# Second layer of a four-layer network: image 0 read and counted ahead, feed-forward and spectrum issued in turns

## The chip, the cores and the metric

The kernel runs on one core of one Trainium2 chip. The metric is device time in microseconds (us) for one execution of the whole network, the median of the timed runs. Five engines work beside each other, each from its own queue: TensorE (PE, with its weight loads listed as PEld), VectorE (DVE), ScalarE (ACT), GpSimd (POOL) and SyncE (SP), which issues most DMAs.

## The reference

Four images of 64 x 64 pixels with 128 channels pass through four layers, each of the form `x = x + layer(group_norm(x))` with 32 groups, all in float32:

```python
def _gn(v, G=32, eps=1e-5):          # mean and variance over pixels and 4 channels
...
x = x + _L0_conv_ref(_gn(x), ...)    # selective scan in four directions over 4096 steps
x = x + _L1_conv_ref(_gn(x), ...)    # the layer of this change
x = x + _L2_conv_ref(_gn(x), ...)    # spectral convolutions with attention over channels
x = x + _L3_conv_ref(_gn(x), ...)    # attention in 7 x 7 windows
```

The second layer takes, along each of the two image axes, a real Fourier transform, keeps 16 modes, multiplies each mode by its own complex 128 x 128 matrix, transforms back, adds the two results, and runs a feed-forward with a layer norm:

```python
def _L1_conv_ref(x, w1, w2, ff_w0, ff_b0, ff_w1, ff_b1, ln_g, ln_b):
    ...
    f1 = jnp.einsum('bixy,ioy->boxy', rfft(xt, axis=-1)[..., :16], cw1)   # axis y
    f2 = jnp.einsum('bixy,iox->boxy', rfft(xt, axis=-2)[:, :, :16], cw2)  # axis x
    h = irfft(f1, axis=-1) + irfft(f2, axis=-2)
    h1 = relu(einsum('bmni,ih->bmnh', h, ff_w0) + ff_b0)                  # 128 to 512
    h2 = einsum('bmnh,ho->bmno', h1, ff_w1) + ff_b1                       # 512 to 128
    return layer_norm(h2, ln_g, ln_b)
```

(The transforms are shown in short; they are unitary, norm 'ortho'.)

## The kernel before

**Layer 0** (`layer0`) takes 73% of the time. Its work is cut into 128 units: 4 images, 4 scan directions, 8 chunks of 512 steps. A unit has 16 steps, one for each state, of about 2.75 us: POOL multiplies `dB`, ACT makes `dA`, DVE scans into `h`, PE transposes `h` (`pt`), ACT copies it (`hT`), and PE multiplies it with `W` into `yT`. PE runs seven steps behind (`LAG`), so after the last unit a loop drains the queue (`while queue or copied: transposed()()`). The order on PE, ACT, DVE and POOL is the order of the program (`tc.manual_schedule`); SP's is left to the scheduler. Work on the side (`Side`) is put into fixed steps: `before` prepares the next image, `after` closes an image in eight bands of 512 pixels. A band reads the summed `y` and the gate `z` back from DRAM (`yf`, `zf`), normalizes, transposes (`pg`), scales (`yg`), multiplies by `z` on POOL, projects (`op`), adds the residual (`xr`) and stores `x1`. The last band of image 3 can begin only when the drain has ended, and it runs in `d.finish`.

**Layer 1** (`layer1`, `layer1_image`) is written image by image; the scheduler orders all engines by its own model, within the limits of the buffers. Its pools are opened when those of layer 0 are released. For each image:

- `load_image` reads x in four DMAs (two buffers `x1`), and `group_norm` makes 32 transposes (`gn_ps`), 8 `bn_stats`, and two small matmuls (`gn_gm`, `gn_gv`) that give scale and offset.
- For each axis: 32 matmuls `pu` with the 96 columns of the transform, copied by ACT with the scale into `U`; 64 matmuls `pg` with `w1` or `w2`, copied by DVE into `G`; 16 transposes `pt`, copied by ACT into `GT`; 16 matmuls `ph`, which DVE copies into `hT` (axis 0) or adds to it (axis 1). Axis 1 uses `xa`, the same image read from DRAM in the other order. `U`, `G`, `xa` and `hT` have one buffer each.
- The feed-forward, in 8 chunks of 512 pixels: 4 matmuls `pf` with bias and relu on ACT (`h1`), 16 matmuls `po`, then layer norm on DVE (`h2`), the sum into x and a store.

In float32 each matmul appears twice in the profile, as two passes, and a transpose once. After image 0, `layer2_weights` loads and combines constants of layer 2. Layers 2 and 3 follow and are not touched, but the pools of layer 2 lie where those of layer 1 lay. L1067 is the helper line through which all of layer 2 is issued.

Of the kernel before, what the change touches and what calls it, by code (L numbers as in the profile page):

```python
# [84 lines left out]
def layer0(sh, A, x_in, x_out, scr):  # L85
# [7 lines left out]
    with ExitStack() as ctx:  # L93
# [28 lines left out]
        xds = [wp.tile([65, CH], F32, name=f"xd{n}") for n in range(2)]  # L122
        for xd in xds:
            nc.vector.memset(xd, 0.0)
            nc.vector.memset(xd[64:65, :], 1.0)
# [12 lines left out]
        zeros = wp.tile([P, WD // P], F32, name="zeros")  # L138
        nc.vector.memset(zeros, 0.0)
# [50 lines left out]
        def opening(bank, steps):  # L190

            waiting = {"dve": [], "act": []}
# [25 lines left out]
            pair = lambda name: tmp.tile([P, 2, CH], F32, name=name, tag="t4", bufs=4)  # L218
            whole = lambda: tmp.tile([P, 2, CH, 4], F32, name="h", bufs=3).rearrange("p s t n -> p (s t n)")
            x = whole().rearrange("p (j d) -> p j d", d=DM)  # L220
            for c in range(NCH):
                nc.sync.dma_start(x[:, 4 * c : 4 * c + 4, :], tiles(x_in(0)[c * CH : (c + 1) * CH, :]))
            for name in ("W00", "W01", "W10", "W11"):
                for g in range(4):
                    nc.sync.dma_start(scr(name)[g].rearrange("(p f) -> p f", p=P), zeros)
# [148 lines left out]

        def after(b, st, later, bands):

            for c in bands:
                yield "l"
                rows = slice(c * CH, (c + 1) * CH)
                y = tmp.tile([P, 4, 2 * P], F32, name="yf", tag="t4", bufs=4)  # L380
                nc.sync.dma_start(y, tiles(scr(f"y2{b % 2}")[rows, :]))
# [38 lines left out]
        def residual(b, rows, xr, op):  # L420
            nc.vector.tensor_tensor(xr, xr, op, ALU.add)
            nc.sync.dma_start(tiles(x_out(b)[rows, :]), xr)
# [10 lines left out]
        def inputs(k, c, u, par, spare):  # L433

            xd, bd, Wd = xds[c % 2], scr(f"B{(NCH * k + c) % 3}"), scr(f"W{k // 2}{par}")
# [13 lines left out]
            def blocks():  # L449
                Ct = tmp.tile([48, 32, 16], F32, name="Ct")[32:48]  # L450
# [95 lines left out]
        def products(G, q, hT):  # L546
# [30 lines left out]
            if G["g"] == 3 and q % 2:  # L577
# [10 lines left out]
                if q == 3:  # L588
                    nc.sync.dma_start(U["dst"](k), y)
# [43 lines left out]
        with tc.manual_schedule(engines=order):  # L633
# [4 lines left out]
            for i, (b, k, c) in enumerate(units):  # L638
# [13 lines left out]
                unit = dict(k=k, pos=pos, rev=rev, pc=pc, u=u, yT=[None, None], started=set(), st=ln_st, dst=dst)  # L652
# [7 lines left out]

                for n in range(NS):
# [74 lines left out]
                elif b == NB - 1 and i % per == 3 * per // 4:  # L736

                    done = [NS * (i + 1 + n) + 8 for n in range(NCH)]
                    sides.append(Side(after(b, ln_st, later, range(NCH - 1, -1, -1)), 8 * 6, done[0], 1, done))
            while queue or copied:  # L740
                transposed()()
# [35 lines left out]
def layer1_weights(sh, A, wp):  # L777
# [3 lines left out]
    nc.scalar.dma_start(w["an"], A["c_an1"])  # L781
    for name in ("w1", "w2"):
        w[name] = wp.tile([P, 16, 2, P], F32, name=name)
        nc.sync.dma_start(w[name], A[name])
    w["ff0"] = wp.tile([P, 4, P], F32, name="ff0")
    nc.scalar.dma_start(w["ff0"], A["ff_w0"].rearrange("i (f k) -> i f k", k=P))
    w["ff1"] = wp.tile([P, 4, P], F32, name="ff1")
    nc.scalar.dma_start(w["ff1"], A["ff_w1"].rearrange("(f k) o -> k f o", k=P))
    w["b0"] = wp.tile([P, 4], F32, name="b0")
    nc.scalar.dma_start(w["b0"], A["ff_b0"])  # L790
    w["rows"] = wp.tile([P, 3, P], F32, name="rows1")
    nc.scalar.dma_start(w["rows"], A["l1_rows"].partition_broadcast(P))
    w["sy"] = wp.tile([P, 256], F32, name="c_sy1")
# [4 lines left out]
def layer1_image(sh, w, pools, x_dram, x_out, x=None):  # L798

    nc = sh.nc  # L800
    big, tmp, small, ps = pools
    if x is None:
        x = big.tile([P, NJ, DM], F32, name="x1")
        load_image(nc, x, x_dram)
    s_, o_ = sh.group_norm(lambda j: x[:, j, :], ps, small, tag="a")
# [3 lines left out]
    hT = big.tile([P, NT], F32, name="hT", bufs=1)  # L809
    for axis in range(2):  # L810

        if axis == 0:
            xa = x
        else:
            xa = big.tile([P, NJ, DM], F32, name="xa", bufs=1)
            xv = x_dram.rearrange("(h w2 w1) d -> w1 h w2 d", w1=2, w2=32)
            for q in range(2):
                nc.sync.dma_start(xa[64 * q : 64 * q + 64], xv[q])
        U = tmp.tile([P, 3, 16, 64], F32, name="U1", bufs=1)
        for g in range(NJ // 4):  # L820
# [8 lines left out]
            )  # L829
        nc.vector.tensor_scalar(U[:, 1, 0, :], U[:, 1, 0, :], o8, None, ALU.add)  # L830

        G = tmp.tile([P, 64, 16, 2], F32, name="G1", bufs=1)
        wm = w["w1"] if axis == 0 else w["w2"]
        for g in range(4):
# [5 lines left out]
            nc.vector.tensor_copy(G.rearrange("p l m c -> p m c l")[:, 4 * g : 4 * g + 4], pg)  # L840

        for g in range(4):
# [4 lines left out]
            GT = tmp.tile([P, 4, P], F32, name="GT1")  # L847
            nc.scalar.copy(GT, pt)
            for q in range(0, 4, 2):
# [13 lines left out]
                else:  # L863
                    hv = hv.rearrange("p h w -> p w h")[:, l0 : l0 + 8, :]
                    nc.vector.tensor_tensor(hv, hv, ph, ALU.add)


    for c in range(NCH):
        h1 = tmp.tile([P, 4, CH], F32, name="h1")
        for f in range(4):  # L870
            pf = ps.tile([P, CH], F32, name="pf", tag="a")
            nc.tensor.matmul(pf, lhsT=w["ff0"][:, f, :], rhs=hT[:, c * CH : (c + 1) * CH], start=True, stop=True)  # L872
            nc.scalar.activation(h1[:, f, :], pf, AF.Relu, bias=w["b0"][:, f : f + 1])  # L873
        po = ps.tile([P, 4, DM], F32, name="po", tag="b")
# [6 lines left out]
        h2 = tmp.tile([P, 4, DM], F32, name="h2")  # L881
# [15 lines left out]
        nc.sync.dma_start(x_out[c * CH : (c + 1) * CH, :].rearrange("(j p) d -> p j d", p=P), xc)  # L897


def load_image(nc, x, x_dram):  # L900
    for q in range(4):
        nc.sync.dma_start(
            x[:, 8 * q : 8 * q + 8, :], x_dram[1024 * q : 1024 * q + 1024, :].rearrange("(j p) d -> p j d", p=P)
        )


def layer1(sh, A, x_in, x_out, l2w, wt):

    tc, nc = sh.tc, sh.nc
    with ExitStack() as ctx:  # L910
        pool = lambda name, bufs, **kw: ctx.enter_context(tc.tile_pool(name=name, bufs=bufs, **kw))
        pools = pool("l1big", 2), pool("l1tmp", 2), pool("l1small", 2), pool("l1ps", 4, space=PSUM)
        wp = pool("l1w", 1)
        x = pools[0].tile([P, NJ, DM], F32, name="x1")
        load_image(nc, x, x_in(0))
# [1162 lines left out]
```

## Time and profile before

| | |
|---|---|
| median of 3 timed runs | 7832.24 us (7831.64 to 7838.32) |
| profiled execution, its own time | 7839.47 us |
| span of the profiled instructions | 7837.7 us |
| layer 0: first to last band | 0 to about 5747 us of the span |
| layer 1: image 0's first spectrum matmul | 5783.1 us |
| layer 1: starts of the four feed-forwards | 5841.6, 5969.4, 6095.5, 6221.7 us |
| layer 2: first load of its input | 6284.7 us |
| busy over the whole span | PE 81%, DVE 86%, ACT 78%, POOL 72% |

All times inside the profile are counted from the start of its span. An average over the whole span says little here: layer 0 keeps DVE, ACT and POOL full, and layer 1 is one fifteenth of the time with PE as its busiest engine. So the stages are read one by one.

### The profile page before, as it was taken

The numbers are of one execution on the slowest core, as the hardware profiler recorded it, in microseconds if no ns is written. First come the engines' busy times: TensorE is split into PE (matmuls) and PEld (weight loads), VectorE is DVE, ScalarE is ACT, GpSimd is POOL, SyncE is SP. The second block draws the span as 40 slices with busy tenths as digits, with TensorE's granted clock in tenths as the row PEclk, the third lists the DMA queues.
The fourth block names the chain that finished last, engine by engine and source line by source line (L and its number), as shares of the span: only waits on it lengthen the run. The fifth ranks groups of instructions, "written<-read, shape, count | busy, mean of one in ns | idle before, by whom it ended". The sixth has DMA issues, their size and how long they took to land. (4 is left out here: it accounts for less than half of the span.)

```text
span 7837.7 us, 141040 instructions
## 1 busy us (share of the span) xinstructions
PE 6346.8 (81%) x52796; PEld 4010.0 (51%) x52796; DVE 6755.1 (86%) x8112; ACT 6108.1 (78%) x9714; POOL 5634.8 (72%) x2574
## 2 busy tenths in 40 slices
PE   7888888878888877888887777787768968687789
PEld 3544444444455444445554444454457756464556
DVE  7999999999999999999999999999955556646678
ACT  7999999999999998999999999999832323314667
POOL 4989999989999998999999999999910013123233
PEclk8999999999999999999999999999989979788899
DMA  6555556545556554555555545555542142231332
GB/s 173 171 163 175 177 174 173 175 154 175 187 172 185 181 171 166 166 183 174 185 175 173 172 152 189 176 174 181 175 106 51 29 120 70 70 107 37 103 96 81
DMA packets 1326912, 1159.93 MB, mean 148 GB/s; under 512 B 694165, under 2 KB 1120753, under 8 KB 1259282
## 3 DMA queue, kind: packets, MB, share of 16 engines
q1 hardware_dynamic: 1324546, 1149.16, 47.7%
q8 instruction: 416, 6.82, 0.4%
q14 instruction: 270, 2.21, 0.1%
q10 hardware_dynamic: 1680, 1.74, 0.1%
HBM read 956.89 MB, written 189.74 MB: 146 GB/s over the span
## 5 line engine op out<-in xcount | busy, mean ns | idle before, releaser
L679 DVE TENSOR_TENSOR_SCAN h<-dA,state,dB 128x512 f32<-128x512 f32 x4096 | 4920.4, 1266 | 201.0 <-POOL dB L673 79.8
L673 POOL TENSOR_TENSOR dB<-du,Bb 128x1024 f32<-128x1024 f32 x2048 | 4810.6, 2385 | 338.2 <-DVE h L679 210.6
L533 PE MATMUL pt<-ident,h 128*128 128x128 f32 x16384 | 2221.9, 279 | 878.9 <-ACT hT L543 863.1
L678 ACT ACTIVATE dA<-delta,A_neg 128x512 f32<-128x512 f32 x4096 | 2761.7, 697 | 159.2 <-DVE h L679 131.3
L533 PEld LDWEIGHTS pt<-ident,h 128*128 128x128 f32 x16384 | 1811.4, 142 | 1930.6 <-ACT hT L543 1708.0
L543 ACT COPY hT<-pt 128x1024 f32<-128x1024 f32 x2048 | 2080.1, 1016 | 163.0 <-PE pt L533 145.1
L568 PE MATMUL yT<-hT,W 128*32 128x256 f32 x16384 | 1378.9, 409 | 1.1 <-ACT hT L543 0.6
L568 PEld LDWEIGHTS yT<-hT,W 128*32 128x32 f32 x16384 | 455.4, 150 | 340.6 <-issue 328.1
L1067 POOL COPY XG<-Xs 64x9 f32<-64x9 f32 (+2 forms) x44 | 10.8, 293 | 758.6 <-ACT Xs L1067 758.6
L164 PE MATMUL cv<-xn,taps 128*128 128x512 f32 x936 | 527.0, 644 | 2.8 <-DVE delta L469 2.8
L1798 POOL TENSOR_TENSOR S<-S,sm 128x784 f32<-128x784 f32 x128 | 191.2, 1494 | 417.4 <-DVE sm L1796 248.0
L472 POOL TENSOR_TENSOR du<-delta,u 128x1024 f32<-128x1024 f32 x128 | 304.7, 2380 | 79.5 <-DVE delta L469 79.4
L460 PE MATMUL dp<-xd,w_dt 65*128 65x512 f32 x512 | 288.7, 646 | 68.4 <-ACT Ct L451 45.9
L443 PE MATMUL xd_ps<-u,w_x 128*48 128x512 f32 x512 | 250.1, 611 | 21.4 <-DVE e L361 15.8
L1805 ACT ACTIVATE S<-S,mx 128x196 f32<-128x196 f32 x512 | 227.9, 448 | 35.4 <-DVE mx L1832 34.9
L164 PEld LDWEIGHTS cv<-xn,taps 128*128 128x128 f32 x936 | 139.2, 188 | 180.6 <-issue 160.5
L873 ACT ACTIVATE h<-pf,b 128x512 f32<-128x512 f32 x128 | 88.0, 687 | 144.9 <-PE pf L872 144.9
L469 DVE SCALAR_TENSOR_TENSOR delta<-delta,dp 128x512 f32<-128x512 f32 x256 | 170.7, 667 | 4.1 <-ACT delta L466 1.1
L1760 PE MATMUL pt<-ident,S 128*98 128x128 f32 x1024 | 164.9, 285 | 3.5 <-POOL S L1798 2.0
L466 ACT ACTIVATE delta<-delta 128x512 f32<-128x512 f32 x256 | 166.0, 649 | 0.0
L460 PEld LDWEIGHTS dp<-xd,w_dt 65*128 65x128 f32 x512 | 76.5, 188 | 173.2 <-ACT Ct L451 98.8
L1067 POOL TENSOR_TENSOR WX<-wr,Xs 128x544 f32<-128x544 f32 x40 | 57.3, 1434 | 148.4 <-issue 62.1
(369 smaller groups left out, 7039.3 us busy)
## 6 DMA issues: line engine op xcount, KB each, us to landing
Bb<-l_B SPq DMA_DIRECT2D x512, 1024.0 KB
W<-l_W SPq DMA_DIRECT2D x512, 256.0 KB
l_y<-y SPq DMA_DIRECT2D x128, 512.0 KB
u<-l_xr SPq DMA_DIRECT2D x64, 512.0 KB
u<-l_xw SPq DMA_DIRECT2D x64, 512.0 KB
y<-l_y SPq DMA_DIRECT2D x56, 512.0 KB
V<-l_v SPq DMA_DIRECT2D x512, 49.0 KB
y<-l_y SPq DMA_DIRECT2D x80, 256.0 KB
```

What stands on the lines that cost most here:

```text
L164: nc.tensor.matmul(pm, lhsT=taps[:, s, t, :], rhs=xn[:, dy : dy + 8, dx : dx + 64], start=(t == 0), stop=(t == 8),)
L443: nc.tensor.matmul(bank["x"], lhsT=w_x[:, s, k, :], rhs=u[:, s, :], start=(s == 0), stop=(s == 1))
L460: nc.tensor.matmul(bank[s], lhsT=w_dt[:, k, s * P : (s + 1) * P], rhs=xd, start=True, stop=True)
L472: nc.gpsimd.tensor_tensor(du, delta, u, ALU.mult)
L533: nc.tensor.transpose(pt[:, j, s, :], G["h"][:, s, t0 : t0 + 32, :].rearrange("p t n -> p (t n)"), sh.ident)
L543: return lambda: nc.scalar.copy(hT, pt.rearrange("p j s d -> p j (s d)"))
L568: nc.tensor.matmul(U["yT"][e][32 * jo : 32 * jo + 32, qo % 2, :], lhsT=U["Ws"][G["g"]][:, :, 4 * q + j], rhs=hT[:, j, :], start=((e, jo) n ...
L673: nc.gpsimd.tensor_tensor(dB, du, B_now[:, q : q + 1, :].to_broadcast([P, 2, CH]), ALU.mult)
L678: nc.scalar.activation(dA, delta[:, s, :], AF.Exp, scale=A_neg[:, k, s, n : n + 1])
L679: nc.vector.tensor_tensor_scan(h[:, s, :, q], dA, dB[:, s, :], state[:, s, n : n + 1], ALU.mult, ALU.add)
L1798: nc.gpsimd.tensor_tensor(Sv, Sv, U["sm"].unsqueeze(2).to_broadcast([P, 4, 196]), ALU.mult)
L1805: nc.scalar.activation(Sn, Sn, AF.Exp, bias=U["mx"][:, n : n + 1], accum_out=sm[:, n : n + 1])
```

## The change

Three things are changed; the rest makes room for them.

**Image 0 ahead.** A pool on the right side of SBUF holds the second layer's first image during the whole of layer 0 (16 KB per partition). Its four parts are read at units 116 to 119. The group statistics are made in the drain loop, one chunk a step, and `group_scale` follows ahead of the last band. The last unit's `y` stays in SBUF for the last band instead of going through DRAM, and the last two bands are stored through ACT's queue. To make room, `xd` and `Ct` get one buffer instead of two, and `zeros` shares a buffer with others (tag `t4`).

**Turns.** `layer1_image` becomes two generators: `layer1_spectrum` yields after each small group of matmuls, `layer1_feed` twice per chunk. `layer1` issues the feed-forward of image b - 1 and the spectrum of image b in 16 turns. `hT` gets two buffers, and the feed-forward issues the `pf` of a chunk ahead of the `po` of the one before. SP now keeps the order of the program within layer 1. All pools of layer 1 wait tile by tile for what lay in their place (`reuse_waits="tile"`) and not for a whole pool.

**Layer 2's constants** (`layer2_weights`) become a generator too; it is stepped along with image 2's spectrum instead of following image 0, its tiles lie on the right where image 0 was, and its loads are all on SP.

```diff
-        xds = [wp.tile([65, CH], F32, name=f"xd{n}") for n in range(2)]
+        xd = wp.tile([65, CH], F32, name="xd")
...
-        zeros = wp.tile([P, WD // P], F32, name="zeros")
...
+            zeros = pair("zeros").rearrange("p s t -> p (s t)")[:, : WD // P]
...
+                if kept:
+                    y = kept.pop()
+                else:
+                    y = tmp.tile([P, 4, 2 * P], F32, name="yf", tag="t4", bufs=4)
+                    nc.sync.dma_start(y, tiles(scr(f"y2{b % 2}")[rows, :]))
...
+            eng = nc.scalar if b == NB - 1 and rows.start <= CH else nc.sync
+            eng.dma_start(tiles(x_out(b)[rows, :]), xr)
...
-                Ct = tmp.tile([48, 32, 16], F32, name="Ct")[32:48]
+                Ct = tmp.tile([48, 32, 16], F32, name="Ct", bufs=1)[32:48]
...
-                if q == 3:
+                if q == 3 and U["last"]:
+                    kept.append(y)
+                elif q == 3:
                     nc.sync.dma_start(U["dst"](k), y)
...
+                if len(units) - 12 <= i < len(units) - 8:
+                    load_part(nc, ahead["x"], x_out(0), i - len(units) + 12)
...
+            def count():
+                for c in itertools.islice(counted, 1):
+                    pt = psx.tile([P, CH], F32, name="gn_ps", tag="x")
+                    for q in range(4):
+                        nc.tensor.transpose(pt[:, q * P : (q + 1) * P], ahead["x"][:, 4 * c + q, :], sh.ident)
+                    nc.vector.bn_stats(st[:, c, :], pt)
+
             while queue or copied:
-                transposed()()
+                copy = transposed()
+                count()
+                copy()
+            for c in range(NCH):
+                count()
+            ahead["norm"] = sh.group_scale(st, psx, ahead["pool"], "x", exp_rstd)
             for d in sides:
                 d.finish(flush_all)
...
+    for name, pool in (("w1", wp), ("w2", wq)):
+        w[name] = pool.tile([P, 16, 2, P], F32, name=name)
...
-    hT = big.tile([P, NT], F32, name="hT", bufs=1)
+    hT = out["hT"] = tmp.tile([P, NT], F32, name="hT", bufs=2)
...
+        if axis == 0:
+            out["xa"] = big.tile([P, NJ, DM], F32, name="xa", bufs=1)
+            xv = x_dram.rearrange("(h w2 w1) d -> w1 h w2 d", w1=2, w2=32)
+            for q in range(2):
+                nc.sync.dma_start(out["xa"][64 * q : 64 * q + 64], xv[q])
...
+    h1_next = first(0)
+    for c in range(NCH):
+        h1 = h1_next
+        if c + 1 < NCH:
+            h1_next = first(c + 1)
+        yield
...
+        with tc.manual_schedule(engines=engines):
+            for b in range(NB + 1):
+                out = {}
+                if b < NB:
+                    spectrum = layer1_spectrum(sh, w, pools, x_in(b), x, norm, out)
+                    pieces = 32 + 9 * (norm is None)
+                else:
+                    spectrum, pieces = iter(()), 0
+                turns = 2 * NCH if b > 0 else 1
+                for n in range(turns):
+                    next(fed, None)
+                    for _ in range(pieces * n // turns, pieces * (n + 1) // turns):
+                        next(spectrum)
+                        next(setup, None)
+                for _ in itertools.chain(spectrum, fed):
+                    pass
+                if b < NB:
+                    fed = layer1_feed(sh, w, pools, x, out["hT"], x_out(b))
+                if b == 1:
+                    ahead["close"]()
+                    right = ctx.enter_context(tc.tile_pool(name="l2set", bufs=1, side="right", reuse_waits="tile"))
+                    w2 = {}
+                    setup = layer2_weights(sh, A, l2w, right, pools["ps"], wt, w2)
+                if b + 1 < NB:
+                    x, norm = pools["big"].tile([P, NJ, DM], F32, name="x1", bufs=2), None
+                    load_image(nc, x, x_in(b + 1))
...
+        early = ExitStack()
+        pool = early.enter_context(tc.tile_pool(name="l1x", bufs=1, side="right"))
+        ahead = dict(pool=pool, x=pool.tile([P, NJ, DM], F32, name="x1"), close=early.close)
```

In this code `engines` is SP alone. A spectrum yields 8 times for `pu`, 4 for `pg` and 8 for `pt` and `ph`, for each of two axes, and 9 times for the statistics where it makes them.

## The prediction

> **What bounds the kernel now.** I read the busy table by stages first, cut where the second layer's stages begin, then the chain of waits across the same stretch, then who waited for whom, then the timeline at both ends. Columns of the first view: window, length, then PE, weight loads, DVE, ACT and POOL busy us with their counts, granted clock, DMA share, GB/s.
>
> ```profile
> 5743.20:5783.10 39.90, 12.44 (x52) 10.60 (x53) 9.14 (x23) 1.28 (x1) 0.00 (x0) 0.54 0.93 219
> 5783.10:5841.60 58.50, 50.51 (x354) 46.75 (x354) 35.61 (x79) 13.87 (x25) 0.00 (x0) 0.96 0.61 119
> ...
> 5969.40:6026.10 56.70, 56.69 (x323) 41.15 (x324) 36.96 (x119) 23.20 (x39) 0.00 (x0) 1.00 0.09 29
> 6026.10:6038.00 11.90, 5.15 (x37) 4.17 (x34) 10.32 (x29) 0.30 (x1) 0.00 (x0) 0.82 0.14 44
> 6038.00:6095.50 57.50, 50.73 (x354) 47.18 (x353) 24.28 (x29) 13.86 (x25) 0.00 (x0) 0.95 0.37 74
> 6095.50:6164.10 68.60, 61.85 (x357) 45.34 (x357) 47.27 (x148) 23.49 (x40) 0.00 (x0) 0.97 0.10 31
> ```
>
> The rows are: the gap between the layers (40 us, DMA 93% busy, PE nearly idle); image 0's spectrum; image 1's feed-forward, with PE busy 56.69 of 56.70 us; the turn to image 2, where DVE finishes the feed-forward and the next statistics; image 2's spectrum; its feed-forward and turn. So the layer is one gap and then PE work with small holes: (57.50 - 50.73) + (68.60 - 61.85) = 13.5 us of PE idle in image 2's 126.1 us. DVE is busy 71.6 us of those, ACT 37.4: neither can bind soon.
>
> ```profile
> 5728.10 2.94 DMA l_y<-y
> 5731.06 3.78 DMA yf<-l_y
> ...
> 5758.39 19.64 DMA x<-x
> 5778.16 1.95 PE gn_ps L60 x8
> 5783.29 9.52 PE pu L823 x64
> ...
> 5811.99 7.13 PE pu L823 x64
> ...
> 5848.47 2.90 PE po L877 x26
> ...
> 5855.48 2.90 PE po L877 x26
> ```
>
> This is the chain (start, length, what). The end of layer 0 writes y out and reads it back (6.9 us), then image 0 is loaded (20 us) and counted before its first matmul at 5783. The same 64 records of pu take 9.52 us after the idle and 7.13 us in the flow. One feed-forward chunk costs 7.01 us.
>
> ```profile
> PE gn_ps L60 <- DMA x<-x: 25.4, 4, 8.9
> ...
> PE gn_gm L71 <- DVE gn_mv L69: 14.8, 4, 5.1
> ...
> PE pf L872 <- DVE hT L865: 9.0, 4, 2.2
> ...
> PE pt L846 <- DVE G L840: 7.7, 7, 1.1
> ...
> PE pg L838 <- DVE U L830: 7.7, 8, 1.0
> ```
>
> These waits (total us, times, longest) are the holes: 25.4 once, at the start; the others return with each image, each at most 5.1 us.
>
> ```profile
> 5708.26 2.36 POOL L673 TENSOR_TENSOR dB<-du,Bb 128x1024 f32<-128x1024 f32 x1
> ...
> 5713.13 1.09 PE L533 MATMUL pt<-ident,h 128*128 128x128 f32 x8 [0.56 <-ACT hT L543]
> ...
> 5743.14 3.78 PE L412 MATMUL op<-w_out,yg 128*128 128x128 f32 x16 [3.29 <-POOL yg L407]
> ```
>
> In the drain of layer 0 PE has 0.56 us free in each 2.25 us step; Bb is last read at 5710.6; the last band ends near 5747.
>
> **The change, part by part.** *Start.* Image 0's 2 MB now come in during units 116 to 119, four transfers of 0.5 MB where the DMA share is about 0.5 to 0.6; they are hidden, and if they pushed a load of Bb or u, each would cost at most its own length (20 us for four at the gap, so 5 us each). Its 32 transposes go into the eight drain steps: four transposes of 0.112 us make 0.45, under the 0.56 free; without that cover all eight would cost 3.6 us. The last product ends at 5727.3, the sum and statistics of y at 5728.9, one more bn_stats (0.70) makes 5729.6, and the chain from aggregate to scale took 3.1 us in the trace (5780.87 to 5783.97). So the scale is there at 5732.7, and pu, which had started 0.9 us before the scale, starts at about 5732 instead of 5783.1: 51 us. I keep 50 for a drain step that overflows. Its weights must be there: by the pools' sizes an and w1 now lie where Bb lay (free at 5710.6), w2 and xa where h lay (free from 5717 and 5726). w1, w2 and xa are 6 MB; at 219 GB/s, the gap's rate, they take 28 us, so w1 is in before 5732 and xa by about 5745, when axis 1 asks for it near 5761. ff0 to c_sy are five issues on ACT's queue, 0.4 to 0.7 us each, among hT copies that leave ACT 1.24 us per step. The other bound: if nothing may pass layer 0's last band, its end at 5746.9 loses the 6.9 us round trip of y and gains 3.8 us of statistics queued ahead of it on DVE, and pu starts at about 5744: 39 us.
>
> *Turns.* From feed-forward to feed-forward the images now take 126 to 128 us, 380.1 us for three (5841.6 to 6221.7). PE's own work in such an interval is 126.1 - 13.5 idle = 112.6, less the slow pu (10.1 against 7.1) = 109.7. With two streams a hole in one can be filled from the other. Not all: 32 pieces are counted for a spectrum that yields 40, so the last eight (pt, ph and the hT sums of axis 1) are issued after the whole feed-forward, and there the 1.1 us wait for G and the 2.2 us wait for hT stay; with 0.7 us for matmuls issued in an order that the data does not keep, 4 us. 113.7 x 3 = 341: 39 us gained. Bounds: 51 (no hole) and below nothing (third rival). What is late next is PE itself. The clock: where PE idles (6026 to 6038) it is 0.82, and the pu behind it is 3 us longer; the 109.7 has this out. The Trainium skill (TensorE: Matmul & The Clock Gate, Part 1: The HAM clock gate) has PE run at half clock for a window of about 3.4 us after an idle window. That is an estimate of 1.7 us lost per hole where the row shows 3; by it three intervals would gain 35 and not 39.
>
> *Waits that are added.* All second-layer DMAs on SP keep program order. xa of the next image stands behind the store of chunk 3, the next x behind the store of chunk 7. Loads of 2 MB land in 10 to 12 us; xa is asked for four turns (about 25 us) after its place in the queue; x lands about when the next feed-forward starts, which has two chunks (14 us) to run before it needs the other stream. I cost both at nothing; if the cover fails, each costs up to 10 us per image, 60 in all. Layer 2's constants move from image 0 to image 2's spectrum: about 16 us of small DVE work (rows of 0.15 to 0.75 us) in an interval where DVE has 40 us free.
>
> *Layer 0.* xd and Ct have one buffer instead of two. Both are written at step 7 of a 44 us unit and read by step 9 and by DMAs whose data the next unit loads at its step 2; nothing waits. zeros takes a t4 buffer until its stores end at 30 us; that buffer is next written near 49.7. Nothing for the three; bound: a 2.5 us stall once.
>
> *End.* By sizes l1big now reaches over layer 2's first big tiles, so their first load waits until the last store has landed (2.5 us by the chain's row for x<-xr); it used to be issued 0.5 us after the last sum. Loss 2.5.
>
> **Sum.** 50 + 39 - 2.5 = 86.5. The profiled span of 7837.7 (execution 7839.5) becomes 7751; the median of the timed runs, 7832.2, lies 7.2 us below that execution, so I predict 7832.2 - 86.5 = 7746. That is 1.1%.
>
> **Rivals.** *Turns bring nothing* (PE stays full only inside the feed-forward, the interval stays at 126): gain 50 - 2.5 = 47, time 7785. For it: feed-forward alone fills PE to 56.69 of 56.70, so interleaving helps only the 13.5 us of holes. Against it: these holes are waits of 1 to 5 us on DVE and ACT, while a chunk of 7 us needs neither. *The start isn't freed* (the layer's first matmuls stay behind the last band): 39 for the start, 30 if xa, the last of the 6 MB, is 9 us late (2 MB at 219 GB/s); with the turns 75.5 or 66.5, time 7757 to 7766. For it: no matmul of the second layer comes ahead of the last band's in this trace. Against it: here they all waited for image 0, whose first part came 8 us after that band. *Slower*: the order on PE is fixed when the program is built, so one late operand holds both streams. Three intervals have 48 turns. A stall of x us in every turn costs 48x on top of 109.7 x 3; the gain of 98.5 (50 + 51 - 2.5) is gone at x = 2.1. The longest steady waits are 1.0 to 2.2 us, so the price exists, but every turn would have to pay it; at 2.6 us the time is 7858. The skill speaks for this rival: the same page (Part 3, What overlaps and what doesn't) has matmuls start and end strictly in order, with only weight loads pulled ahead. No row here shows a matmul that passed another; by that rule at the trace's 1.0 us for U it would be 48 us lost, 7782, and still faster.
>
> **How the numbers follow.** Forecast 0.68; turns bring nothing 0.13; start not freed 0.09; slower 0.06; and 0.04 that gains and stalls cancel. A difference of 0.2% (15.7 us) is about what a measurement of this kernel tells from none. Faster 0.90, same 0.04, slower 0.06. The range: below, 51 + 51 - 2.5 and image 0's pu at the warm 7.1 us (2.4 less) make 7730, and 3 us are added for the spread of the runs; above, turns that bring nothing (7785) with a start at 39 (7796) and the same spread.
>
> **What would show it.** Right: pu of image 0 near 5732 to 5735, its bank statistics inside the drain, no l_y round trip before the last band; three starts of feed-forwards 110 to 118 us apart; PE idle under 6 us per interval; the first xg load near 6198. Wrong at the start: PE waiting for w1, or pu after 5744. Wrong in the turns: waits of PE on DMA of x or xa, or on hT, over 5 us per image. Wrong altogether: layer 0's last POOL dB far from 5710.

## The result, and the profile after

| | before | after |
|---|---|---|
| median in the first comparison, 4 runs each | 7835.28 us (7831.64 to 7839.69) | 7785.97 us (7783.61 to 7793.69) |
| profiled execution, its own time | 7839.47 us | 7787.28 us |
| span of the profiled instructions | 7837.7 us | 7785.3 us |
| layer 0: last dB on POOL | 5708.26 us | 5712.21 us |
| first pu of image 0, counted from that dB | 74.9 us | 37.6 us |
| first feed-forward, counted from that dB | 133.3 us | 94.8 us |
| feed-forward to feed-forward, three intervals | 127.9, 126.1, 126.2 us | 116.9, 123.6, 118.6 us |
| last feed-forward to layer 2's first load | 63.0 us | 66.4 us |
| from the last dB to that load | 576.4 us | 520.3 us |

The changed kernel is faster: ratio 0.9939, 95% interval 0.9921 to 0.9956. In a second comparison on another occasion (x9 below) it was 0.9934, 0.9921 to 0.9946. The forecast was 7746. The gain is 49 us by the medians and 56 us by the stretch that the change touches, where 86.5 were forecast.

The same table by stages for the kernel after, columns as in the prediction. Cuts are the last dB, the first pu, the four feed-forwards and layer 2's first load.

```profile
5712.21:5749.76 37.55, 26.34 (x207) 19.01 (x206) 14.56 (x31) 10.93 (x15) 4.70 (x3) 0.79 0.19 65
5749.76:5807.03 57.27, 49.24 (x354) 44.99 (x353) 26.49 (x38) 13.16 (x24) 0.00 (x0) 0.99 0.55 130
5807.03:5923.89 116.86, 109.93 (x708) 90.18 (x709) 68.39 (x177) 38.62 (x66) 0.00 (x0) 0.99 0.26 61
5923.89:6047.49 123.60, 114.42 (x712) 93.04 (x712) 80.71 (x231) 37.67 (x65) 0.00 (x0) 0.94 0.26 62
6047.49:6166.05 118.56, 111.63 (x709) 90.77 (x709) 68.30 (x177) 37.56 (x65) 0.00 (x0) 0.97 0.16 36
6166.05:6232.50 66.45, 56.32 (x320) 40.82 (x320) 41.87 (x136) 23.63 (x40) 0.00 (x0) 0.95 0.11 32
```

The gap of 40 us with idle engines is gone. In the three intervals the length less PE's busy time is 6.9, 9.2 and 6.9 us, against 13.0, 13.5 and 13.5 before. And PE's busy time itself differs, 109.9, 114.4 and 111.6 us for the same matmuls (four small transposes of layer 2's constants in the second aside), with a granted clock of 0.99, 0.94 and 0.97.

The chain of waits after (start, length, what):

```profile
5743.80 2.35 POOL yg L411
5746.19 3.79 PE op L416 x16
...
5755.18 22.87 DMA xa<-x
...
5797.56 9.42 DVE hT L901 x8
5807.03 7.13 PE pf L913 x16
```

The round trip of y, the load of image 0 and its statistics have left the chain. What stands there instead is the last band of layer 0 (yg, op), which ends at 5749.97; pu starts at 5749.76, on its heels (PE's timeline; the ends of matmuls are modelled, so the two may overlap a little):

```profile
5749.76 4.42 PE L851 MATMUL pu<-c_an,x 128*128 128x96 f32 x32
```

The load of xa is on the chain, but PE had the first axis to do meanwhile and waited 0.67 us for it. At the end of image 0's spectrum DVE's eight sums into hT are on the chain for 9.4 us, and PE is idle for the last 2.2 of them; the same 2.2 us stand before every later feed-forward.

What PE waited for in the three intervals (total us, times, longest):

```profile
PE pt L881 <- DVE G L874: 9.4, 6, 1.9
PE pf L913 <- DVE hT L901: 6.7, 3, 2.2
PE gn_gv L78 <- DVE gn_d L76: 3.1, 3, 2.6
PE pg L872 <- DVE U L859: 2.9, 3, 1.0
PE ph L888 <- ACT GT L883: 0.9, 3, 0.3
```

No wait for gn_gm and gn_ps is left: the holes of the group statistics are filled by the other image's feed-forward. Those of the spectrum's own chain (U, G, GT, hT) all stay. No wait on a DMA appears: x and xa were there in time.

### The profile page after: what moved, and what is told of

Same layout as the page of the kernel before. It is cut to its first block, busy times and chain, and to the rows that moved or that the text cites. A ratio compares the mean times of both kernels' runs of the same rounds, so it can differ in the third digit from the quotient of the medians.

```text
span 7785.3 us, 141007 instructions
## 1 busy us (share of the span) xinstructions
PE 6346.5 (82%) x52796; PEld 4005.2 (51%) x52796; DVE 6741.9 (87%) x8109; ACT 6109.7 (78%) x9715; POOL 5636.4 (72%) x2574
## 5 line engine op out<-in xcount | busy, mean ns | idle before, releaser
L1886 POOL TENSOR_TENSOR S<-S,sm 128x784 f32<-128x784 f32 x128 | 191.1, 1493 | 415.3 <-DVE sm L1884 350.9
L448 PE MATMUL xd_ps<-u,w_x 128*48 128x512 f32 x512 | 250.9, 613 | 23.6 <-DVE e L360 18.1
L914 ACT ACTIVATE h<-pf,b 128x512 f32<-128x512 f32 x128 | 87.7, 687 | 117.3 <-PE pf L913 99.2
```

The lines of the kernel that those rows point to most:

```text
L448: nc.tensor.matmul(bank["x"], lhsT=w_x[:, s, k, :], rhs=u[:, s, :], start=(s == 0), stop=(s == 1))
```

## The experiments

All stretches below are counted from the last dB of the same profile, because layer 0's end moves by 12 us from run to run (x8). The changed kernel is the base of every edit, unless another is named.

### The turns: x1, x2, x3

**x1_pieces** counts the pieces right.

```diff
-                    pieces = 32 + 9 * (norm is None)
+                    pieces = 40 + 9 * (norm is None)
```

> The count of pieces is 40 + 9 instead of 32 + 9, so that the last eight pieces of a spectrum (pt, ph and the sums into hT of axis 1) are issued inside the 16 turns and not behind the whole feed-forward. Theory A (those eight pieces stand bare at the end of each image, with 1.9 us of pt waiting for G, 0.3 of ph and 2.2 of pf waiting for hT): the three intervals from feed-forward to feed-forward, now 116.9, 123.6 and 118.6 us, fall by about 4 us each, and the time falls by 12 us to about 7774. Theory B (the first chunk of the next feed-forward needs the last sum into hT wherever its pieces are issued, and the holes are those of a chain that runs U, G, GT, hT through three engines): the holes move but do not go, intervals within 1.5 us of what they are, time 7782 to 7790.

Measured: 7781.16 us (7776.76 to 7797.44, 4 runs), ratio to before 0.9927 (0.9913 to 0.9942); intervals 114.3, 125.1 and 117.3 us, 356.7 in sum. That is 2.3 us under the changed kernel's 359.0, where theory A wanted 12; it is less than the 6 us by which these sums differ between profiles that have the same turns (see x9), and PE's idle time did not fall (23.6 us over the three, 23.0 before the edit). One line of its waits on PE, over the same intervals:

```profile
PE pf L913 <- DVE hT L901: 14.0, 4, 3.9
```

From the second feed-forward on, pf now waits 3.9 us instead of 2.2 for the last sum into hT. The last chunk's po does stand among the last pieces, but DVE takes most of that chunk's layer norm among the last four sums. The holes moved: theory B.

**x2_constants** moves layer 2's constants by one image.

```diff
-                if b == 1:
+                if b == 2:
                     ahead["close"]()
```

> The constants of layer 2 are stepped along with image 3's spectrum instead of image 2's. Theory A (the second interval is 5 to 7 us longer than the other two because the constants' DVE work sits in the chain of the group statistics there, PE idles 2.6 us at gn_gv and the clock falls): the second interval falls from 123.6 to about 118, the third rises from 118.6 to about 124, and the sum stays at 359 within 2 us. Theory B (the long interval belongs to image 2's loads or to the place in the run, not to the constants): intervals stay at 117, 124, 119.

Measured: intervals 118.4, 116.9 and 122.2 us, 357.5 in sum; PE's wait at gn_gv is 0.3 us in the second and 2.4 us in the third. Theory A: the hole goes with the constants (PE's idle time is 6.9, 6.9 and 9.0 us). That is 2.1 us of the 4 to 5 by which the interval is longer; the rest is PE's busy time, which the next section takes up.

**x3_no_turns** issues one stream behind the other.

```diff
-                    for _ in range(pieces * n // turns, pieces * (n + 1) // turns):
-                        next(spectrum)
-                        next(setup, None)
-                for _ in itertools.chain(spectrum, fed):
-                    pass
+                for _ in itertools.chain(fed, spectrum):
+                    next(setup, None)
```

> The feed-forward of an image is issued whole, and the next image's spectrum behind it, with buffers, loads ahead and everything else as in the changed kernel. Theory A (the turns give 21 us and the start gives the rest): the intervals go back to 126 to 128 us, 380 in sum, and the time is 7786 + 21 = 7807; the start (first pu near 5750, first feed-forward near 5807) stays. Theory B (the scheduler, which orders PE by its own model in this layer, interleaves the two streams by itself once hT and the loads allow it, so that the order of issue hardly matters): intervals 117 to 122, time 7786 to 7795.

Measured: 7829.48 us (7818.78 to 7838.01, 10 runs), ratio to before 0.9987 (0.9977 to 0.9996). Intervals 126.7, 145.9 and 126.9 us. The first and third are within 1 us of the kernel before where no constants fall into the interval (126.1 and 126.2), and their waits stand in the same places; in the first:

```profile
PE gn_gm L71 <- DVE gn_mv L69: 3.9, 1, 3.9
PE gn_ps L831 <- DVE gn_st L832: 2.5, 1, 2.5
...
PE gn_gv L78 <- DVE gn_d L76: 0.8, 1, 0.8
```

These 7.2 us are what the turns fill: idle time of PE 14.1 us in this interval, 6.9 with turns. PE's busy time falls too, from 112.5 to 109.9 us. The scheduler does not interleave the streams by itself, so theory B falls. The time is 22 us above theory A's for a reason of its own: in the second interval the constants are now stepped with the feed-forward, and PE waits 14.05 us for Wpv at the first of their transposes (pw). (In the kernel before, where they followed image 0, that interval was 1.7 us longer than the other two.)

### The clock behind a hole

The second interval is the longest, and its hole at gn_gv (2.59 us, for gn_d on DVE) explains only part of it. Below is the table by windows for the changed kernel right behind that hole; the clock is the third number from the right.

```profile
5953.50:5956.00 2.50, 2.50 (x11) 2.50 (x12) 2.07 (x11) 0.38 (x2) 0.00 (x0) 0.50 0.03 7
5956.00:5961.00 5.00, 5.00 (x8) 1.95 (x8) 2.35 (x11) 2.68 (x5) 0.00 (x0) 0.65 0.18 52
```

And for x4, whose layer 1 has the same order there and the same hole of 2.59 us:

```profile
5950.80:5953.30 2.50, 2.50 (x14) 1.78 (x15) 2.27 (x13) 1.07 (x3) 0.00 (x0) 1.00 0.03 7
5953.30:5958.30 5.00, 5.00 (x33) 3.80 (x32) 4.97 (x17) 3.92 (x8) 0.00 (x0) 1.00 0.18 52
```

With the clock at 0.50 and 0.65 the eight rows of pf behind the hole take 5.53 us; at 1.00 they take 3.62. x4's second interval is 119.3 us with 9.3 us of idle time, the changed kernel's 123.6 with 9.2. So some 4 us of that interval are the clock alone, and whether they are paid is not decided by the program. Over its three intervals x4 has (length, then PE's busy time):

```profile
sum 352.78, PE 329.69 PEld 269.62 DVE 217.28 ACT 113.84 POOL 0.00; mean PE 109.90 PEld 89.87 DVE 72.43 ACT 37.95 POOL 0.00
```

The changed kernel's sum is 359.02 us with 335.98 of PE busy: 6.3 us more for the same matmuls in the same turns, with the same idle time of 23 us. x4's granted clock is 0.99 in all three intervals, the changed kernel's 0.99, 0.94 and 0.97. The same holds for the 2.2 us before each pf: the first 16 rows behind it take 7.13 us in some intervals and 8.83 in others.

### The start: x4, x5, x6, x12

**x4_band_first** takes four steps of the last band ahead of image 0's group scale.

```diff
+            for d in sides:
+                for _ in range(4):
+                    flush_all()
+                    d.step()
             ahead["norm"] = sh.group_scale(st, psx, ahead["pool"], "x", exp_rstd)
```

> The last band of layer 0 gets its first four steps (sums of the statistics, factor, normalized y, both transposes) ahead of the group scale of image 0, instead of behind it. Theory A (image 0's first matmul is held by the end of the last band on PE, and that band is held by the 3.6 us chain of the group scale, 5732.8 to 5736.4): the last op ends near 5746 instead of 5750, pu starts right behind it near 5746, and as the loads of w2 and xa wait for the store of that band, all of the start moves with it: first feed-forward at about 5803.5 instead of 5807.0. Theory B (pu is held by its own scale or weights, not by the band): pu stays at 5749 to 5750 although op ends earlier.

Measured: first pu 36.4 us after the last dB (37.6), first feed-forward 92.7 (94.8). pu again starts when op ends (op 5744.77 for 3.68 us, pu 5748.29). The move is 1.2 us and not 4: the band's second yg was ready to run on ACT but stood behind gn_s there (gn_s 5741.14 and 5741.43, yg 5741.54). Theory A in kind, with a step in the wrong place.

**x5_loads_early** lets w2 and xa follow w1, and puts the five small loads behind them on SP.

```diff
     w["ff0"] = wq.tile([P, 4, P], F32, name="ff0")
-    nc.scalar.dma_start(w["ff0"], A["ff_w0"].rearrange("i (f k) -> i f k", k=P))
...
+    nc.sync.dma_start(w["w2"], A["w2"])
+    load_turned(nc, w["xa"], x_dram)
+    nc.sync.dma_start(w["sy"], A["c_sy1"])
+    nc.sync.dma_start(w["ff0"], A["ff_w0"].rearrange("i (f k) -> i f k", k=P))
...
```

> The loads of w2 and of xa of image 0 come right behind w1 in the program, and the five small constants (ff0, ff1, b0, rows, c_sy), which ACT issued ahead of its first U, come behind them on SP. In the changed kernel w2 is issued 38 us after w1 (5753.6), because completions of DMAs are counted on eight semaphores in turn and w2 has the one of the last band's store, and xa stands behind w2. Theory A (the last band holds the loads, but PE hardly waited for them: 0.67 us; what the start loses beside the band is ACT's five issues, 3.1 us ahead of the first U): w2 is issued near 5720, xa lands before 5760, the first U starts about 3 us sooner after the first pu, and the stretch from layer 0's last dB to the first feed-forward falls from 94.8 to 91 or 92 us. Theory B (xa is what holds the start): the stretch falls by 6 us or more.

Measured: SP's own timeline, the first line of the changed kernel, the second of x5 (start, length, what; two issues in the first, the second of which came 38 us after the first):

```profile
5714.99 38.64 SPq L808 DMA_DIRECT2D w<-in_w  x2
```

```profile
5723.36 0.33 SPq L815 DMA_DIRECT2D w<-in_w  x1
```

The loads are some 30 us sooner, and the start gains 2.0 us against the first profile of the changed kernel: pu 37.5 us after the last dB as before, the feed-forward at 92.8. Theory A: the loads were held by the last band's store, but PE hardly waited for them. The first U starts 1.95 us after the first pu instead of 4.1, since ACT's five issues no longer stand ahead of it; what PE gains by that is less. Five more profiles with the unedited start (x1, x2, x3, x7, x9) have 56.3 to 56.4 us from pu to the feed-forward, the first had 57.3, x5 has 55.3. So about 1 us is the edit's, and the other was the first profile's own (its 0.67 us for xa among it).

**x6_early_and_band** is x5 with five steps of the band, and a flush, ahead of the scale.

```diff
+            for d in sides:
+                for _ in range(5):
+                    flush_all()
+                    d.step()
+            flush_all()
             ahead["norm"] = sh.group_scale(st, psx, ahead["pool"], "x", exp_rstd)
```

> As x5, and the last band gets five of its steps (up to the product with z on POOL) ahead of image 0's group scale, so that no step of the band stands behind the scale on ACT, as one did in x4. Theory A (one chain: the last y, the band, then pu): from last dB to first pu 34 us instead of 37.5, and with the early loads 87 to 88.5 us from last dB to the first feed-forward instead of 94.8. Theory B (what the band gains is lost behind the scale, which is now on the path): first pu no sooner than 36.4 us after the last dB, as in x4, and 90 us to the feed-forward.

Measured: pu 34.5 us after the last dB, feed-forward at 89.1. PE's timeline:

```profile
5746.28 3.78 PE L416 MATMUL op<-w_out,yg 128*128 128x128 f32 x16 [1.77 <-POOL yg L411]
5749.85 7.57 PE L865 MATMUL pu<-c_an,x 128*128 128x96 f32 x64
```

Theory A: the band's op ends 34.7 us after the last dB (37.7 in x5), and pu moved by the same 3 us.

**x12_no_last_band** leaves the band out.

```diff
                 if kept:
-                    y = kept.pop()
+                    kept.pop()
+                    xr = tmp.tile([P, 4, DM], F32, name="xr", tag="t2", bufs=4)
+                    nc.sync.dma_start(xr, tiles(x_in(b)[rows, :]))
+                    nc.sync.dma_start(tiles(x_out(b)[rows, :]), xr)
+                    continue
```

> As x5 (loads early), and the last band of layer 0 for image 3 is left out: its 512 pixels are stored without what layer 0 adds to them, so that no step of it stands between the group scale of image 0 and pu. It shows whether the prediction's 50 us were there if pu had not stood behind that band. Theory A (the band alone holds the start; scale, weights and xa are in time): first pu 24 to 26 us after the last dB (37.5 in x5), and 80 to 82 us from the last dB to the first feed-forward (92.8). Theory B (with the band gone, pg waits for w1 or the second axis for xa, the last of 6 MB): pu comes early but the first feed-forward stays at 86 us or more.

Measured: pu 23.5 us after the last dB, the first feed-forward at 80.2. PE's timeline where layer 1 begins:

```profile
5735.34 0.56 PE L78 MATMUL gn_gv<-gn_d,gmat 128*128 128x1 f32 x2 [0.79 <-DVE gn_d L76]
5735.76 9.70 PE L864 MATMUL pu<-c_an,x 128*128 128x96 f32 x64
```

pu starts right behind the group scale's last matmul and 51.4 us sooner than before (74.9 - 23.5). In the times of the profile before that is 5731.8 (5708.3 + 23.5), where the prediction had "about 5732". Weights and xa were in time. So the 50 us of the forecast were there; the place of the last band on PE took 12 to 14 of them. No run keeps the band and issues pu ahead of it, so what that order would give is open.

### The end, and layer 0: x7, x8

**x7_const_l2big** has two edits: constants from the eleventh piece on, and tile by tile waits for layer 2's big pool.

```diff
                         next(spectrum)
-                        next(setup, None)
+                        counted += 1
+                        if counted > 10:
+                            next(setup, None)
...
-        tmp, small, big = pool("l2tmp", 1), pool("l2small", 1), pool("l2big", 1)
+        tmp, small = pool("l2tmp", 1), pool("l2small", 1)
+        big = ctx.enter_context(tc.tile_pool(name="l2big", bufs=1, reuse_waits="tile"))
```

> Two edits in different places. The constants of layer 2 are combined in the same image's spectrum, but from its eleventh piece on, behind the group statistics. And the pool of layer 2's big tiles waits tile by tile for what lay in its place, not for the whole pool of layer 1. Theory A (the wait of PE for gn_d and the fall of the clock behind it come from constants in the statistics' chain on DVE; the first load of layer 2 waits for the last store of layer 1): the second interval falls from 123.6 to 118 or 119, with no hole of 2.6 us at gn_gv, and the stretch from the last feed-forward's start to the first load of xg falls from 66.4 to 63 or 64 us. Theory B (constants cost the same wherever they stand in the spectrum, since DVE is late all along; the load waits for the data itself): second interval 122 to 124, stretch 66.

Measured: second interval 119.5 us. The hole at gn_gv is 0.3 us, but one of 2.6 us stands at pt, which waits for G: the constants take DVE's time there instead, and the idle time of the interval is 8.8 us where it was 9.2. So theory B has the mechanism. Theory A's number is no evidence for the edit: x4 and x5, where the constants stand as in the changed kernel, have 119.3 and 119.6 us, because the clock stayed up in them. At the end the changed kernel's chain is the first fence, x7's issue on SP the second:

```profile
6229.30 0.70 DVE x L945
6230.02 2.27 DMA x<-x
...
6232.49 4.19 DMA xg<-x
```

```profile
6230.55 5.79 SPq L1158 DMA_DIRECT2D xg<-x  x5
```

In the changed kernel the load of xg waits for the last store to land, 2.5 us after the last sum. In x7 the last sum ends at 6230.06 and the load is issued 0.5 us later: 2.0 us gained. The stretch of 66.1 us hides that, because in this run the last feed-forward began with a slow pf (8.83 us); with a slow pf and without the edit it is 68.2 us (x1, x2, x4, x5, x6).

**x8_before_again** is the kernel before, unchanged.

> The kernel before, unchanged, profiled once more, to see how layer 0's end spreads from run to run. Theory A (layer 0 is the same work in both kernels; its last dB came 4 us later in the profile of the changed kernel by the spread of runs, since its thousandth dB was 3.7 us late and its three thousandth was not): the last dB lies anywhere from 5708 to 5721, and the stretch from last dB to first xg load is 576 to 577 us, as in the first profile of this kernel. Theory B (single buffers for xd and Ct or the loads of image 0 cost layer 0 4 us): last dB at 5708 within 0.5 us.

Measured: last dB at 5718.1 us (5708.3 in the first profile), from there to xg 575.9 us. Twelve profiles of kernels with the changed layer 0 have it from 5708.9 to 5720.7. Theory A: the 4 us by which layer 0 was later in the first pair are within the spread. A difference of a few us either way stays open. The parts of this second profile differ from the first: first pu at 72.6 us after the last dB and first feed-forward at 131.1 (74.9 and 133.3), and 64.6 us from the last feed-forward to xg (63.0), with a slow pf. The gains by part below are taken from the first pair and are good to about 2 us.

### Together: x9, x10, x11

**x9_changed_again** is the changed kernel, timed beside the next two.

> The changed kernel, unchanged, timed beside the two kernels below. Theory A (the gain is that of the stretch from layer 0's last dB to the first xg load, 576.4 to 520.3 = 56 us, and the 49 us of the first comparison were short by the spread of layer 0's end): 50 to 58 us under the kernel before. Theory B (layer 0 is some 4 to 7 us slower in the changed kernel): 45 to 50 us.

Measured: 7787.56 us (7774.37 to 7794.92) against 7836.20: 48.6 us by the medians, and 42 to 62 by the ratio's interval. The time does not tell the two theories apart. From last dB to xg 516.7 us; the intervals were 115.2, 122.4 and 118.6 with the same idle times as in the first profile (7.0, 9.2, 6.9), so the sum is 356.1 us instead of 359.0 for the same program, and all of the difference is in PE's busy time. x4, x5, x6 and x12, whose turns are those of the changed kernel, have 352.8, 353.1, 357.7 and 356.1 us, with 23.0 to 23.4 us of idle time: a spread of 6 us that no edit to the turns made.

**x10_four_mends** is x6 and x7 together (their diffs).

> Four edits together: loads early and constants of the layer on SP (x5), five steps of the last band ahead of the group scale (x6), layer 2's constants combined from the eleventh piece on and its big tiles waiting tile by tile (x7). Theory A (the edits act in different places and add up): last dB to first feed-forward 89 us (94.8 in the changed kernel), three intervals 350 to 356 us (359.0), last feed-forward to xg 63 to 66 us (66.4), so 505 to 511 us from last dB to xg instead of 520.3, and a time 10 to 15 us under the changed kernel. Theory B (the places are coupled by the clock: a hole that closes in one place lets a pf run slow in another): 514 to 516 us, as in x5, x6 and x7 each, and 5 us under the changed kernel.

Measured: 7780.69 us (7774.95 to 7786.43), ratio to before 0.9926 (0.9913 to 0.9940); start 88.7, intervals 118.4, 123.0 and 116.9 (358.3), end 66.1, 513.1 us in all. The start gave what it should, the intervals nothing: the second has a hole of 3.5 us at pt for G, from the constants, and the idle time of the three is 23.3 us as it was. By its number this is theory B; the coupling by the clock that it names is not shown, as PE's busy time lies within the spread seen without the edits.

**x11_tail** adds the count of x1 and a pause in the feed-forward.

```diff
+        if c == NCH - 1:
+            yield
         row = lambda n: w["rows"][:, n, :].unsqueeze(1).to_broadcast([P, 4, DM])
```

> As x10, with the full count of pieces (x1) and one more pause in the feed-forward: the last chunk's po is issued ahead of the spectrum's last pieces and its layer norm on DVE behind them. Theory A (the end of a spectrum is carried by DVE: eight sums into hT of 1.18 us; po of the last chunk fills PE there, and in x1 the layer norm of that chunk stood before the sums and made pf wait 3.9 us): pf waits 2.2 us or less, each interval falls to 112 to 115 us, three of them to 338 to 345 us, and the time is 10 us under x10. Theory B (the layer norm is then late for the next image's statistics, which need DVE too, so that the wait only moves to gn_gm): three intervals 350 to 357 us, time within 3 us of x10.

Measured: 7774.37 us (7770.19 to 7778.28), ratio to before 0.9918 (0.9904 to 0.9931); start 88.4, intervals 114.9, 120.6 and 115.4 (350.9), end 66.1, 505.5 us in all. One line of its waits on PE over the intervals:

```profile
PE pf L927 <- DVE hT L915: 10.7, 4, 2.8
```

pf waits 2.2 to 2.8 us instead of the 3.9 of x1. The statistics of the last chunk's layer norm still stand among the last four sums, but of its later steps only 0.7 us instead of 1.8. The statistics of the next image did not suffer (no wait at gn_gm). Theory A in kind, at less than its size: 7.4 us in the intervals and 6.3 in the time, under x10. Of the 7.4 us 3.5 are idle time of PE (19.8 us against 23.3); the other 3.9 are busy time and within its spread. This is the fastest whole version run: 13 us under the changed kernel in the same comparison by the medians, though the ranges of single times overlap.

## Why the prediction was right or wrong

**Right.** The direction, the three places, and most mechanisms: image 0's load and statistics cost layer 0's drain nothing (its steps stay 2.25 us with four transposes more in each), loads of x and xa are covered in every turn, the round trip of y is gone, layer 0 keeps its time within its spread, and PE's own work in an interval is 109.9 us (109.7 was the estimate) where the clock stays up. Three of the signs that the forecast named went against it: pu came after 5744, the starts of the feed-forwards were not all 110 to 118 us apart (116.9, 123.6, 118.6), and PE's idle time per interval was over 6 us. No single turn had a stall like the slower rival's. That the measured 7786 is the time named for the rival "turns bring nothing" (7785) is chance: the turns gave 21.1 us where that rival has none, and the start 38.5 where it has 50.

**The start: 50 forecast, 38.5 measured** (133.3 - 94.8). The step that failed is the choice between its two values. "pu starts at about 5732" assumed that the layer's first matmul may pass the last band; the other bound, "if nothing may pass layer 0's last band", came to 39 and is what happened. PE keeps the order in which the program was built, and there the band stands ahead of pu. The operands were in time: ACT ends the group scale at 5736.2, 24.0 us after the last dB, and the forecast had 24.4. x6 moved the band by 3 us and pu moved by 3 us; x12 removed it and pu came 51.4 us sooner. The prediction gave this case a chance of 0.09 and argued that "here they all waited for image 0", which is true of the trace of before and says nothing of the order that is built once image 0 is there. The rule of the Trainium skill that matmuls start strictly in order (TensorE: Matmul & The Clock Gate, Part 3: What overlaps and what doesn't) was weighed for the turns only; the rows of x6 and x12 agree with it here, at the start. The second fear in that rival, xa late by 9 us, was not paid: xa and w2 were issued 38 us late, yet PE waited only 0.67 us for them. The forecast had the five issues on ACT's queue among the hT copies and gave them no cost; they came behind the last band's store and held the first U by 2 us, which cost PE about 1 us (x5).

**The turns: 39 forecast, 21.1 measured** (380.1 - 359.0). Two terms of the sum were too small. "4 us" of holes per interval was 6.9, 9.2 and 6.9: 11.0 us too little over three. The forecast's list had 1.1 us of pt and 2.2 of pf, both of axis 1. Measured they are 1.9 and 2.2, and the list left out 1.2 us of pt in axis 0, 1.0 of pg for U, 0.3 each of ph and gn_gv, and the 2.6 us that the constants bring. "109.7" was 109.9, 114.4 and 111.6: 6.9 us over three. Together 18 us, which is the whole difference. The second term is the clock: with the same turns and the same holes x4 has 329.7 us of PE busy, 3 x 109.9, so the forecast's 109.7 is right where the clock stays up. Of the 18 us, then, 11 come back in every profile with these turns; the rest lies between 0.6 us (x4, x5) and 6.9. That the miscount of pieces costs the eight bare pieces was half wrong: x1 puts them inside the turns and PE's idle time stays, as DVE, not PE, carries the end of a spectrum; x11 takes 3.5 us of idle time out, once some of DVE's layer norm is moved too. "Layer 2's constants ... in an interval where DVE has 40 us free" was the wrong sort of argument: the total was free, but the constants stood in the statistics' chain (x2: 2.1 us of idle time wherever they go, and with the clock 4 to 5 us there).

**The end: a loss of 2.5 forecast, 3.4 measured.** Waiting for the last store is 2.0 of it (2.5 us from the last sum to the load instead of 0.5; x7). The rest lies ahead of the store: pf is now issued a chunk ahead, so the last two po run back to back and the layer norms of the last two chunks mix on DVE. From the end of the last po to the end of the last sum it is 7.6 us (6222.4 to 6230.0); before it was 5.8 (6278.4 to 6284.2).

**The sum.** 38.5 + 21.1 - 3.4 = 56.2, the measured stretch (576.4 - 520.3), against 86.5. In the time 49 us arrived. The 7 us between the two are no larger than the spread of layer 0's end and of the single times, and x9 can't tell them from none. What follows layer 2's first load spreads as well: the twelve profiles with the changed layer 0 have 1544.1 to 1558.7 us from there to the end of the span, the two of the kernel before 1553.0 and 1552.3.

The Trainium skill (TensorE: Matmul & The Clock Gate, Part 1: The HAM clock gate) has the clock set by a window of about 3.4 us that runs freely, without regard to when a kernel starts. That agrees with the same hole of 2.59 us being followed by a clock of 0.50 in one run and 1.00 in another; no run here shows the window itself. The page also has the clock fall after an idle window of that length. Here the lower clock followed holes of 2.2 and 2.6 us, which are shorter; the measurement decides. What else than a hole such a window counts as idle, no run here shows.

## What to carry to other kernels

When work is moved ahead of a barrier, read which instructions stand before it in the order that is built for its engine, not only which operands are ready: a serial tail of small steps on several engines (here 14 us for one band of 512 pixels) holds everything behind it on PE. Interleaving two streams fills the holes where one stream waits and the other has work, and leaves those at the end of a stream's own chain; there the engine that carries the chain must be relieved, and work that is free in total is not free inside it. Count holes by the list of waits, one line for each, and allow for the clock behind every hole of 2 us or more: here between nothing and 3 us (from gn_gv to the end of the eight pf 4.6 us in x4, 7.6 in the changed kernel).

## What the hardware showed that was not expected

- The clock behind a hole of 2.59 us fell to 0.50 in one profile and stayed at 1.00 in another with the same order of instructions; 16 rows of pf behind a hole of 2.2 us took 7.13 or 8.83 us. For the same turns the three intervals summed to 352.8 to 359.0 us in six profiles with equal idle times.
- Layer 0's end, after 5.7 ms of the same work, varies by 12 us from run to run (5708.3 to 5720.7 in the fourteen profiles, both kernels), which is more than most of the effects studied here; the program behind layer 2's first load varies by 15 us. Only stretches counted from a mark within the same profile could tell them apart.
- One late DMA can hold loads that have nothing to do with it. The load of w2 stood 38 us on SP until the store of layer 0's last band, issued by ACT, had landed. In the trace the completions of all 3884 DMAs are counted on eight semaphores, 485 or 486 on each, and w2 has that store's. With another order of the loads (x5) w2 was issued 5.5 us after w1; there two of the small loads (ff0, ff1) waited 6.0 and 9.2 us for stores of layer 0 instead.
